# Three wo products between the third and fourth z product, gathers an expert ahead, and pumped work in finer steps spread by VectorE's share

## The chip, the cores and the metric

The kernel runs on one core of a Trainium2 chip. The metric is the device time of one execution in microseconds (us). PE is TensorE (matmuls; PEld is its weight load), DVE is VectorE, ACT is ScalarE, POOL is GpSimd, and SP is the queue that issues most of the DMAs. Instructions of one engine run in the order in which they stand in its program.

## The reference

The input `x` is 8 sequences of 1024 rows of 256 floats. Two blocks follow each other, each added to its input after a layer norm. The first is a gated scan, the second a mixture of experts in which each row goes to two of eight experts, with at most 256 rows for an expert and sequence.

```python
def gated_scan(x):                       # x: [8, 1024, 256], after a layer norm
    h = rmsnorm(x) * gamma
    q, kv, a = split(h @ w_qkva.T, 3)
    y = associative_scan(sigmoid(a), kv) # y[t] = a[t] * y[t-1] + kv[t]
    return q * y

def moe(x):                              # 8 groups of 1024 rows, after a layer norm
    raw = softmax(x @ router_w)          # 8 experts; top 2, capacity 256 a group
    dispatch, combine = gating_top2(raw, C=256)
    inp = einsum('GSEC,GSM->EGCM', dispatch, x)
    hid = gelu(inp @ w0) * (inp @ w1)    # hidden width 1368
    out = hid @ wo
    return einsum('EGCM,GSEC->GSM', out, combine)

x = x + gated_scan(layernorm(x))
x = x + moe(layernorm(x))
```

## The kernel before, in words

**Blocks, units and sets.** The eight sequences are worked in four blocks of two (`n` = 0 to 3). A unit is one expert in one block (`(n, e)`, 32 of them). Its hidden width of 1368 is cut into six sets (`s` = 0 to 5), five of 256 and one of 88. So there are 192 sets, and `run_set` (L836) writes one.

**The products of a set.** The products with `w0` and `w1` are made as one 2x2 block product by seven multiplications instead of eight (Strassen's scheme in Winograd's form). They need sums of weight blocks (`row_sums`, L649, four adds on POOL, written one set ahead), and sums of the gathered inputs (`column_sums`, L632, on DVE, once a unit). Four of the seven are added up in one PSUM bank, `z`, one after the other, and ACT copies the bank out after each of the first three (`sn`, L869, L881, L889); the next product into `z` waits for the copy. `pa` takes one product and `pb` two. L875, L891, L898 and L827 (`first_sum`) on DVE put them together; two gelus stand on ACT (L890, L830). L891 reads `pb` between its first and its second product, and L898 reads `z`, after which the next set may write it. In sets 0 to 4 each of the seven is four PE instructions, in set 5 two.

**The wo products.** The product with `wo` is made by seven multiplications as well (`out_work`, L771), two sets later. They are the work with which `run_set` fills the time that PE would wait: `products()` stands in five places (after the first z, after `pa`, after the second z, after the third z, after the fourth z), and `shares` (L854 to L861) says how many go to each. One such product is two PE instructions (L753). In the set after a set 5 (so in s=1) there are only four. After these, `join_outputs` (L791) adds up the four banks `y0` to `y3` in three parts on DVE; the products of s=2 write the same banks.

**Pumps.** All other work, that of later blocks' scan, norms and gates and the combining of rows of the block before, is cut into steps and handed out by `pump()`, which stands twice in each set: between the first `pb` product and the third z (half 0), and at the set's end (half 1). A block has 96 pumps, and `plan` says which steps each one runs. `unit_steps` (L196) makes the scan's and the norms' steps, `gate_steps` (L322) those of the top-2 gating, `combine_steps` (L483) the fetches and adds of outputs. Steps are spread evenly by their number over the first 88 pumps.

**The bank `aside`.** Steps and `between` that need PE put their result into one PSUM bank, `aside` (`ps_a`, L66): `h_channels`, `x_channels` (four transposes each, then a copy on ACT, L190), `gate_a`, `scan`, `mix` (projections, read by ACT or DVE), `to_tokens` (L270, read by DVE at L276), `router` (L303), `positions` and `tokens`, the transposes of `input_channels` (L627) and those of `output_rows` (L819, the tile `pt_y`).

**Gathers.** `gather_unit` (L609) fetches the rows of a unit by four indirect DMAs from POOL's queue. For the next expert it is called in the first pump of s=0. `between()` (L1021) runs after the fourth z: `input_channels` transposes the gathered rows of the next unit in s=3 and s=4, and `output_rows` writes out the unit before in s=2 and s=5.

In the main loop the order of all engines is the order written (`tc.manual_schedule()`). Ahead of it, up to some 131 us, a first part does the scan and the gates of the first block with only SP's order fixed.

## Time and profile before

| what | value |
|---|---|
| median of 3 runs | 2111.84 us (2111.2 to 2115.47) |
| the profiled execution | 2110.05 us |
| its span, first to last instruction | 2108.2 us |
| mean granted TensorE clock | 0.986 |
| PE busy / PE weight loads busy | 2007.9 / 1609.5 us |
| DVE / ACT / POOL busy | 1370.5 / 681.8 / 1223.4 us |
| DMA moved | 228.87 MB, mean 109 GB/s |

A line of the profile gives the source line, the engine, the operation, what is written and read, the shape and a count. In the timeline the first two numbers are the start and the length in us; runs of equal instructions are merged, and in square brackets stands how long the engine had been idle and what ended that. Matmuls overlap in the pipeline, so the start of one to the start of the next is what it takes of PE. In the list of waits a line gives who waited for whom, the us in total, how often, and the longest.

### The profile page before, as it was taken

Reading aid. Unit: us, or ns where it says so; the run is one execution under the profiler, and the core shown is the slowest. Engines: PE = TensorE matmul, PEld = TensorE weight load, DVE = VectorE, ACT = ScalarE, POOL = GpSimd, SP = SyncE. Lnnn points to the kernel's source line nnn. Section 1 sums busy time; section 2 is a strip of 40 time slices with the busy share of each in tenths; the row PEclk is TensorE's granted clock in tenths of the full one; section 3 lists DMA queues with packets and bytes.
Section 4 is the critical chain, followed back from the end, with each engine's and each line's share of the span. In section 5 each row is a group of like instructions: output and inputs, shape, how many; then the busy total and the mean of one; then the engine's idle time right before and its main releaser. Section 6 shows DMA issues by size and latency. Waiting matters only on the chain.

```text
span 2108.2 us, 27798 instructions
## 1 busy us (share of the span) xinstructions
PE 2007.9 (95%) x9352; PEld 1609.5 (76%) x9352; DVE 1370.5 (65%) x2617; ACT 681.8 (32%) x1286; POOL 1223.4 (58%) x1754
## 2 busy tenths in 40 slices
PE   8899999999999999999999999999999999999958
PEld 4567877777787778787778877787778888878847
DVE  4665666667766575757765666666776667666425
ACT  3333333332333333243233333333323333333311
POOL 3346555546455666657646566666556666767463
PEclk9989999999999999999999999999999999999989
DMA  5223333323224434343423333443333334344351
GB/s 171 80 89 90 91 90 106 103 93 106 78 77 125 115 101 150 88 123 118 123 81 120 109 100 117 120 124 112 111 110 111 116 105 119 100 141 120 97 165 46
DMA packets 224077, 228.87 MB, mean 109 GB/s; under 512 B 32448, under 2 KB 215744, under 8 KB 223936
## 3 DMA queue, kind: packets, MB, share of 16 engines
q1 hardware_dynamic: 211104, 193.51, 31.1%
q0 software_dynamic: 12288, 33.57, 5.4%
q8 instruction: 76, 1.25, 0.3%
q14 instruction: 65, 0.53, 0.1%
q10 hardware_dynamic: 544, 0.01, 0.0%
HBM read 185.61 MB, written 41.42 MB: 108 GB/s over the span
## 4 chain that ended last, share of the span: by engine, by line
PE 85%; DVE 9%; issue 2%; ACT 2%; POOL 1%; DMA 0%; another core or an unknown queue 0%; SPq 0%; ACTq 0%; DVEq 0%; POOLq 0%
PE z L701 29%; PE acc L753 21%; PE pb L701 14%; PE pa L701 7%; PE pa L237 2%; PE pkv L237 2%; PE pq L237 2%; PE py L733 2%; PE px L627 1%; PE pl L303 1%; PE pt_y L819 1%; ACT sn L889 1%; PE po L270 1%; DVE hid L834 1%; PE pc L591 1%
## 5 line engine op out<-in xcount | busy, mean ns | idle before, releaser
L657 POOL TENSOR_TENSOR sb<-w 128x256 f32<-128x256 f32 x188 | 133.0, 708 | 504.9 <-PE pb L701 501.4
L701 PE MATMUL z<-tb,sb 128*128 128x256 f32 (+1 forms) x1408 | 371.8, 383 | 3.3 <-ACT sn L881 3.3
L701 PEld LDWEIGHTS z<-tb,sb 128*128 128x128 f32 (+1 forms) x1408 | 256.1, 187 | 63.9 <-issue 18.2
L891 DVE TENSOR_TENSOR hid<-sn,pb 128x512 f32<-128x512 f32 x192 | 122.6, 639 | 244.0 <-ACT sn L889 206.6
L869 ACT COPY sn<-z 128x512 f32<-128x512 f32 x192 | 105.6, 550 | 439.2 <-PE z L701 409.3
L753 PE MATMUL acc<-tw,so 128*128 128x256 f32 x900 | 244.4, 381 | 0.0
L701 PE MATMUL z<-tb,w 128*128 128x256 f32 (+1 forms) x704 | 200.8, 404 | 40.7 <-ACT sn L889 23.9
L827 DVE TENSOR_TENSOR c<-sn,pb 128x512 f32<-128x512 f32 x192 | 123.1, 641 | 168.5 <-PE pb L701 158.7
L753 PE MATMUL acc<-hid,wo 128*128 128x256 f32 x840 | 216.2, 380 | 0.0
L875 DVE TENSOR_TENSOR c<-sn,pa 128x512 f32<-128x512 f32 x192 | 122.2, 637 | 139.1 <-PE pa L701 129.8
L701 PE MATMUL pb<-xT,sb 128*128 128x256 f32 (+1 forms) x704 | 187.2, 385 | 21.1 <-DVE hid L891 21.1
L889 ACT COPY sn<-z 128x512 f32<-128x512 f32 x192 | 105.6, 550 | 287.9 <-PE z L701 258.2
L881 ACT COPY sn<-z 128x512 f32<-128x512 f32 x192 | 105.6, 550 | 287.4 <-PE z L701 273.0
L701 PEld LDWEIGHTS z<-tb,w 128*128 128x128 f32 (+1 forms) x704 | 118.9, 187 | 99.8 <-ACT sn L889 69.4
L701 PE MATMUL z<-xT,w 128*128 128x256 f32 (+1 forms) x704 | 189.8, 388 | 4.8 <-DVE hid L898 4.6
L701 PE MATMUL pa<-xT,w 128*128 128x256 f32 (+1 forms) x704 | 183.5, 379 | 0.6 <-ACT hT L190 0.6
L701 PE MATMUL pb<-tb,sb 128*128 128x256 f32 (+1 forms) x704 | 183.3, 379 | 0.0
L753 PEld LDWEIGHTS acc<-hid,wo 128*128 128x128 f32 x840 | 160.1, 191 | 23.1
L753 PEld LDWEIGHTS acc<-tw,so 128*128 128x128 f32 x900 | 162.3, 191 | 18.2
L701 PEld LDWEIGHTS pb<-xT,sb 128*128 128x128 f32 (+1 forms) x704 | 130.8, 189 | 47.7 <-DVE hid L891 23.9
L701 PEld LDWEIGHTS z<-xT,w 128*128 128x128 f32 (+1 forms) x704 | 126.2, 188 | 50.3 <-DVE hid L898 20.2
L660 POOL TENSOR_TENSOR sb<-w,sb 128x256 f32<-128x256 f32 x188 | 157.5, 838 | 0.0
(175 smaller groups left out, 3771.0 us busy)
## 6 DMA issues: line engine op xcount, KB each, us to landing
w<-in_L_ffn_w_kernel_dram SPq DMA_DIRECT2D x320, 256.0 KB
wo<-in_L_ffn_wo_kernel_dram SPq DMA_DIRECT2D x160, 256.0 KB
y<-ot SPq DMA_DIRECT2D x62, 256.0 KB
xt<-in_L_attn_x_dram SPq DMA_DIRECT2D x16, 512.0 KB
x<-xt SPq DMA_DIRECT2D x16, 512.0 KB
xn<-xn SPq DMA_DIRECT2D x16, 512.0 KB
xc<-x SPq DMA_DIRECT2D x16, 512.0 KB
out_dram<-xc SPq DMA_DIRECT2D x12, 512.0 KB
```

The costliest lines, as they stand in the source:

```text
L237: nc.tensor.matmul(pp, lhsT=wT[:, k, c * P : (c + 1) * P], rhs=t["hT"][:, k, :], start=(k == 0), stop=(k == KC - 1),)
L657: eng.tensor_tensor(s1, a21, a22, ALU.add)
L660: eng.tensor_tensor(s4, a12, s2, ALU.subtract)
L701: nc.tensor.matmul(ps[:hs, i * CAP : (i + 1) * CAP], lhsT=a[:, i * hs : (i + 1) * hs], rhs=b, start=first and i == 0, stop=True, skip_grou ...
L733: nc.tensor.matmul(po[:, hh * D : (hh + 1) * D], lhsT=st.hid[:hs, gl, i, hh * P : (hh + 1) * P], rhs=wos[st.j][:hs, i, :], start=(s == 0 a ...
L753: nc.tensor.matmul(ys[n, e, i][:, half * CAP : (half + 1) * CAP], lhsT=lhsT, rhs=rhs, start=fresh, stop=True, skip_group_check=True,)
L827: nc.vector.tensor_tensor(st.c12, st.snap1, st.cut(st.pb), ALU.add)
L869: A.copy(snap0, zz)
L875: V.tensor_tensor(c11, snap0, st.cut(p_a), ALU.add)
L881: A.copy(st.snap1, zz)
L889: A.copy(snap2, zz)
L891: V.tensor_tensor(st.h2[: st.hs, 1, st.wide], snap2, st.cut(p_b), ALU.add)
```

## The change

It has four parts. `shares` changes so that three wo products stand after the third z in the usual sets, and one after the fourth; s=1 and s=2 get other shares too, and in s=1 `between()` stands ahead of the fourth z, and `join_outputs(2)` ahead of `first_sum`. The rows of the expert after the next are gathered in the first pump of s=5 (so those of the next one lie ready when a unit begins), and `input_channels` moves from s=3 and 4 to s=1 and 3 in the units where the rows are there in time. Steps are cut finer: both norms into halves, `top`, `counts` and `places` into parts, the one-hots into fours. And each step has a weight for VectorE's time; a pump also has a load from the joins, the column sums and the adds of `combine_steps`, and the steps are handed out so that the running sum of both keeps to an even line.

```diff
-        def first_norm():
+        def first_norm(half):
+            if half == 1:
+                first_rows(half)
+                return
...
-        def second_norm():
+        def second_norm(half):
...
+        def each(w, f):
+            return [weigh(w, lambda c=c: f(c)) for c in range(2)]
+
+        before_mixer = each(12, first_moments) + each(12, first_norm) + each(3, h_channels)
+        mixer = [f for fs in zip(each(5, gate_a), each(13, scan), each(7, mix)) for f in fs]
+        mixer += each(7, to_tokens)
+        after_mixer = each(12, second_moments) + each(10, second_norm) + each(3, x_channels)
+        after_mixer.append(weigh(3, router))
...
-        steps = [softmax, softmax_sum, lambda: top(0), lambda: top(1), counts, positions, places]
+        steps = [weigh(12, softmax), weigh(9, softmax_sum)]
+        steps += [weigh(10, lambda r=r, q=q: top(r, q)) for r in range(2) for q in range(2)]
+        steps += [weigh(13, lambda q=q: counts(q)) for q in range(2)]
+        steps += [weigh(7, positions), weigh(9, places), weigh(9, kept),
+                  weigh(6, output_places), weigh(20, slot_tokens)]
         for gl in range(GB):
-            steps += [lambda gl=gl, q=q: one_hot(gl, q) for q in range(2)]
-            steps.append(lambda gl=gl: tokens(gl))
+            steps += [weigh(13, lambda gl=gl, q=q: one_hot(gl, q)) for q in range(4)]
+            steps.append(weigh(6, lambda gl=gl: tokens(gl)))
...
         if st.s == 1:
-            shares = [2, 2, 0, 0, 0]
+            shares = [1, 2, 1, 0, 0]
...
-            shares = [0, 0, 3, 2, 2] if st.s == 2 else [2, 0, 1, 2, 2]
+            shares = [0, 2, 1, 3, 1] if st.s == 2 else [2, 0, 1, 3, 1]
...
         products()
+        if st.s == 1:
+            between()
         st.mm(z, a22, t4, False)
         V.tensor_tensor(st.h2[: st.hs, 0, st.wide], zz, c11, ALU.mult)
-        between()
+        if joined:
+            join_outputs(*joined, 2)
+        if st.s != 1:
+            between()
         products()
         st.mm(p_b, s4, b22, False)
         first_sum(st)
         if joined:
-            join_outputs(*joined, 2)
             hid_sums(last, 0)
...
+            load = [12 * (k % (2 * NS) in (2, 3)) + 7 * (k % (2 * NS) in (9, 10))
+                    for k in range(PUMPS)]
...
             if n > 0:
                 for i, (fetch, add) in enumerate(combine_steps(n - 1)):
-                    plan.setdefault(13 + i * 14 // 3, []).append(fetch)
-                    plan.setdefault(15 + i * 14 // 3, []).append(add)
+                    at_pump(13 + i * 14 // 3, fetch)
+                    at_pump(15 + i * 14 // 3, add, 11)
+            if n + 1 < NB:
+                steps = list(token_work[n + 2])
+                share = (sum(f.weight for f in steps) + sum(load[: PUMPS - 8])) / (PUMPS - 8)
+                done = 0.0
+                for k in range(PUMPS - 8):
+                    done += load[k]
+                    while steps and done + steps[0].weight / 2 <= share * (k + 1):
+                        done += steps[0].weight
+                        at_pump(k, steps.pop(0))
...
+                later = (n, e + 2) if e + 2 < NE else (n + 1, 1)
+                if half == 0:
+                    if j == 0:
+                        gather_unit(0, 1)
+                    if s == NS - 1 and e + 2 != NE and later in units:
+                        gather_unit(*later)
                 if nxt in units:
-                    if half == 0 and s == 0 and e + 1 < NE:
-                        gather_unit(*nxt)
...
-                if s in (3, 4) and nxt in units:
-                    input_channels(*nxt, s - 3)
+
+                slots = (3, 4) if nxt[1] == 0 or nxt == units[1] else (1, 3)
+                if s in slots and nxt in units:
+                    input_channels(*nxt, slots.index(s))
```

## The prediction

> **What bounds the kernel now.** I read the page first: who is busy and who carries the chain.

> ```profile
> PE 2007.9 (95%) x9352; PEld 1609.5 (76%) x9352; DVE 1370.5 (65%) x2617; ACT 681.8 (32%) x1286; POOL 1223.4 (58%) x1754
> ...
> PE 85%; DVE 9%; issue 2%; ACT 2%; POOL 1%; DMA 0%; another core or an unknown queue 0%; SPq 0%; ACTq 0%; DVEq 0%; POOLq 0%
> ```

> PE carries the chain and runs its program in the order written, so only time in which PE stands still, and PE work itself, move the end. The change adds no PE work. So I looked for where PE stands still: the waits, then the timeline of a unit that has no pumped work (block 3).

> ```profile
> PEld z L701 <- ACT sn L889: 69.4, 152, 1.1
> ...
> PE z L701 <- ACT sn L889: 23.9, 33, 0.7
> ...
> PE pb L701 <- DVE hid L891: 21.1, 17, 3.0
> ...
> PE pt_y L819 <- DVE xt L276: 4.7, 2, 2.4
> ```

> ```profile
> 1621.62 1.03 PE L701 MATMUL z<-tb,sb 128*128 128x256 f32 x4
> 1622.48 1.03 PE L753 MATMUL acc<-tw,so 128*128 128x256 f32 x4
> 1623.38 1.13 PE L701 MATMUL z<-tb,w 128*128 128x256 f32 x4
> 1624.35 0.59 PE L753 MATMUL acc<-tw,so 128*128 128x256 f32 x2
> ...
> 1631.38 1.10 PE L701 MATMUL z<-tb,sb 128*128 128x256 f32 x4
> 1633.21 1.13 PE L701 MATMUL z<-tb,w 128*128 128x256 f32 x4 [0.73 <-ACT sn L889]
> 1634.18 1.03 PE L701 MATMUL pb<-xT,sb 128*128 128x256 f32 x4
> ```

> Starts are what counts: a group x4 lasts 0.86 us from its start to the next one (0.215 an instruction), a wo product (x2) 0.43. In the first set (s=0) two wo products lie between the third and the fourth z product, and from 1621.62 to 1624.35 are 2.73 us where twelve instructions need 2.58: some 0.14 lost at the fourth z, which waits for the ACT copy of the third. In the second set (s=1) nothing lies between: 1.0 lost. Read so, set by set, the timeline gives these stalls of PE: fourth z 0.14 us in 121 sets (s = 0, 2, 3, 4) and 1.00 in each s=1; second z of s=2 0.146 x30; third z of s=1 0.20 x13; first z after s=5 up to 0.54 (19 sets, 7.6 us), after s=1 0.26 (24 sets).

> The rest is VectorE come too late to L891, and here the timeline shows why:

> ```profile
> 1021.15 0.59 PE L753 MATMUL acc<-tw,wo 128*128 128x256 f32 x2
> ...
> 1023.61 0.29 DVE L445 TENSOR_TENSOR tn<-m,kr 128x128 bf16<-128x128 f32 x1
> 1023.82 0.68 DVE L891 TENSOR_TENSOR hid<-sn,pb 128x512 f32<-128x512 f32 x1
> ...
> 1024.55 1.13 PE L701 MATMUL pb<-xT,sb 128*128 128x256 f32 x4 [2.81 <-DVE hid L891]
> ```

> The step `places`, some 20 instructions in one pump, stands ahead of L891. Such stalls: `places` 3.1, 3.1 and 3.4 us at the second pb and 2.6 just behind it; `top`, `one_hot` or an add in a pump of s=1 (1.1, 1.1, 1.0, 0.6, 0.6); and twice `one_hot` (8 instructions), after which the wait for L276 at pt_y and what follows costs 4.1 us each. In s=5 VectorE is late nearly always (12.8 us in 12 sets): that set is short and holds the column sums. All stalls together, summed from the starts, are some 110 us between 131 and 2020 us.

> **The change, part by part.** The sum is made against the profiled execution, 2110.05 us with a span of 2108.2; the median of the runs shown is 2111.84, so I carry the difference over to that.

> *Three products between third and fourth z.* Cover grows from 0.86 to 1.28 us; the wait needed 0.14 more. In 118 sets (the last two units keep their shares) 118 x 0.14 = 16 us gone. What it takes away is one product (0.43) between the fourth z and the next first z, which waits for L898. In a quiet set L898 ends 3.04 us after the last start of the third z, 3.32 with the later fourth z; the next z then comes at 3.66 in s=0 and 4: 0.2 to spare. In about one such set in six VectorE is later than that: 3 us lost. The next nearest wait, second pb for L891, keeps its cover (three products and z in either order).

> *s=2 and s=1 shares.* s=2 gets two products ahead of its second z (0.146 x30 = 4.4 gone; one is left before the third z, 1.28 us of cover where 1.07 is used); s=1 gets one ahead of its third z (0.20 x13 = 2.6 gone). That s=2 may start its products early rests on `join_outputs(2)` coming before `first_sum`. It puts two adds (0.68 each) ahead of L827 on VectorE; behind L827 are the gelu on ACT and the hid sums, and the next L875 comes after the same row of instructions as before. Free; without that cover 0.2 x31.

> *Transposes moved into s=1.* In 27 units (not those before an expert 0, nor the first and the last) the first `input_channels` moves from s=3 to between third and fourth z of s=1: four transposes, 0.43 us from start to start, in a wait of 1.00. 27 x 0.43 = 11.6. Twice the pump just before holds `scan`, whose bank VectorE frees only 1.98 us after PE's last start: there nothing is won but 0.3 lost. I take 10.

> *Gathers an expert ahead.* Four indirect DMAs on POOL (0.98 us and 0.3 between) move from s=0 to the first pump of s=5. The buffers are free by then (second `input_channels` in s=3 or 4). Queued behind them on POOL are row sums for s=1, some 5 us later than now: they end about 4 us before the second z of s=1 wants them. Free; today's row for that wait is `PEld z L701 <- POOL sb L658`, 4.7 us in all, which I hold as its price if the cover is gone. [...] The trace has 128 of these gathers at a mean of 980 ns beside a VectorE that is busy 65%, so nothing is lost; I go by the row.

> *Finer steps, spread by weight.* Steps ahead of one L891 are now at most about 25 weight units (two half moments 2.3 us, or two scaled rows and four one-hots); pumps with that much outside s=1 and s=5 show no stall today. In s=1 at most a scan or an add stays, which stalls 0.08 at most today. Of 12.2 (`places`), 4.6 (s=1) and 8.2 (pt_y) I take 22 as gone. s=5 stays: adds, half norms and `slot_tokens` still fall into its stretch; 0. The SP stores and loads that move with the steps (x1, xn, the next x) are read tens of us later; 0.

> *What spreading by VectorE's share costs.* This is the term that speaks against it. All pumped PE steps, and the transposes of `between`, share one PSUM bank, `aside`. Today each pump holds one step. By weight, a step that is cheap for VectorE (transposes 3, router 3) hardly counts, so they bunch. I worked the plan out from the rule and weights: of 140 pumped steps that use the bank, 40 now stand directly behind another in the same pump, where it was none. Then PE stands until the first one's bank is read:

> ```profile
> 906.51 0.60 PE L187 MATMUL pt_h<-ident,h 128*128 128x128 f32 x4
> ...
> 906.95 1.03 PE L701 MATMUL z<-tb,sb 128*128 128x256 f32 x4
> 907.15 0.59 ACT L190 COPY hT<-pt_h 128x512 f32<-128x512 f32 x1 [0.38 <-PE pt_h L187]
> ```

> Here PE goes on with another bank at 906.95; for the same bank it must await the copy, which ends at 907.74, and a waited-for start costs some 0.15 more (so much lies between a copy's end and the fourth z's start): 0.94 us. Ahead of another stand: h and x transposes 23 times (0.94: 21.6); router 7 (copy done 0.48 after the last start: 0.5 each, 3.5); to_tokens 6 (L276 ends 1.43 after the last start, median: 1.4 each, 8.4); mix 3 (1.1: 3.3); tokens once (0.6). Sum 37. The bounds: nothing, where another wait would have stood there anyway, and 1.9 (the mean of to_tokens, when VectorE is behind) for each, 76; I take 37, each by its own row. [...] By the only such waits that the trace has, at pt_y, one would count none.

> *Pumps left empty.* First z after s=5 waits 0.54 unless the pump before it has PE work; that is now missing in 23 units for 19, and after s=1 in 28 for 24: 3 us lost with rounding up.

> *First 131 us and the end.* Norms in halves change no count of instructions; 0, within 3. The 20 us in which PE stands between 2032 and 2056 lie in the last unit, whose pumps don't change; 0. One product later in its s=1 saves 0.9.

> Sum: 16 + 4.4 + 2.6 + 10 + 22 + 0.9 = 56 won; 3 + 37 + 3 = 43 lost; 13 won. 2111.8 - 12 or 13: 2099.

> **Rivals.** *The bank decides (slower).* One mechanism: bunched steps on `aside`. 56 won against 6 of other losses leaves 50; from 1.25 us a pair the change loses. For: 16 of the pairs are in a pump at the end of a set, where readers on VectorE stand behind L827 and the hid sums, and ACT may be in a gelu (0.63). Against: today's rows are steady at 0.90. At 1.7 a pair: 68 + 6 - 56 = 18 slower, 2130.
> *VectorE stays late.* The steps are finer but the queue is the same, and new heavy pumps or the thinner cover before the next first z take half of the 22 back: 56 - 11 - 43 = 2 won, 2110. For: s=5 is late whatever stands there. Against: the big stalls all follow one long step.
> *The bank is free.* Half of the 40 fall where PE waits anyhow: 56 - 24 = 32 faster, 2080. For: the waits for L898 before a first z are in just those places. Against: they are small (0.26 to 0.54).

> **How the numbers follow.** Forecast 0.58 (faster), bank free 0.08 (faster), VectorE late 0.10 (no change), bank decides 0.24 (slower). A measurement of this kernel can tell 0.2%, about 4 us, from no change. The range 2082 to 2122 leaves out the lower half of "bank free" and the upper half of "bank decides".

> **What would show it.** In the waits after: `z <- ACT sn` at the fourth z nearly gone except in s=1, there about 0.57 each; `pb <- DVE hid` left in s=5; new rows of PE waiting at pt_h, pt_x, pl, po, pq for hT, xnT, logits and xt, some 40 times and 37 us. I am wrong if those rows are far from 37, if fourth z still waits 0.14, or if stalls over 1.5 us at the second pb remain outside s=5.

## The result, and the profile after

The changed kernel takes 2114.29 us (median of 20 runs, 2111.85 to 2119.91), the kernel before 2113.7 beside it (20 runs): a ratio of 1.0008, with a 95% interval of 1.0001 to 1.0015. Within the 0.2% that counts as no change, the time is the same. 2099 was forecast.

The page after, who is busy and who carries the chain:

```profile
PE 2001.1 (95%) x9352; PEld 1628.4 (77%) x9352; DVE 1375.3 (65%) x2617; ACT 683.7 (32%) x1286; POOL 1230.2 (58%) x1754
...
PE 84%; DVE 8%; issue 3%; ACT 2%; DMA 1%; POOL 1%; another core or an unknown queue 1%; SPq 0%; ACTq 0%; DVEq 0%; POOLq 0%
```

Nothing is to be seen here: PE still carries 84% of the chain. The list of waits (who waited for whom, us in total, how often, longest), here for the main loop alone (131 to 2007 us), shows that the waits are others. Source lines have moved: the products of a set are now L737, ACT's copy of the third z is L925, VectorE's L891 and L898 are L927 and L936.

```profile
PE pb L737 <- DVE hid L927: 11.7, 14, 2.3
PE z L737 <- ACT sn L925: 10.0, 27, 0.7
PE po L285 <- ACT xnT L190: 4.7, 7, 0.7
PE z L737 <- DVE hid L936: 3.9, 15, 0.3
PE pt_x L187 <- ACT hT L190: 3.4, 5, 0.7
PE pq L252 <- ACT xnT L190: 3.4, 5, 0.7
PE ptok L498 <- DVE oneh L488: 2.8, 3, 2.1
PE pl L322 <- ACT hT L190: 2.7, 4, 0.7
...
PE pt_h L187 <- DVE xt L291: 2.4, 3, 0.8
PE pa L252 <- DVE xt L291: 2.4, 3, 0.8
```

The rows of `po`, `pt_x`, `pq`, `pl` and `pt_h` are the forecast's new rows, with its partners; `pa` behind `to_tokens` (`xt`) belongs to them, though the forecast didn't name it. The timeline shows the gain and the loss in one set:

```profile
201.32 1.03 PE L737 MATMUL z<-tb,sb 128*128 128x256 f32 x4
202.19 1.46 PE L789 MATMUL acc<-tw,so 128*128 128x256 f32 x6
203.48 1.03 PE L737 MATMUL z<-tb,w 128*128 128x256 f32 x4
...
205.64 0.60 PE L187 MATMUL pt_h<-ident,h 128*128 128x128 f32 x4
206.92 0.65 PE L187 MATMUL pt_x<-ident,xn 128*128 128x128 f32 x4 [0.68 <-ACT hT L190]
208.25 0.65 PE L285 MATMUL po<-ident,oT 128*128 128x128 f32 x4 [0.68 <-ACT xnT L190]
208.74 1.03 PE L737 MATMUL z<-xT,w 128*128 128x256 f32 x4
```

Ten instructions lie between 201.32 and 203.48, 2.16 us, which is 10 x 0.215: the fourth z waits no longer. But each group of transposes comes 1.28 and 1.33 us after the one before, where four take 0.44. Two stalls of 0.84 and 0.89 in one pump give back what a dozen fourth z products have won.

Summed from the starts of PE's instructions, set by set, PE stands in the main loop (from the first set to the last unit) for:

| where PE stands, us | before | after |
|---|---|---|
| fourth z (for ACT's third copy) | 49.1 | 19.5 |
| second and third z | 7.9 | 1.5 |
| second pb (for L891, now L927) | 25.8 | 17.2 |
| first z (for L898, now L936) | 14.6 | 17.7 |
| at a step on the bank `aside` | 5.4 | 39.5 |
| PE's instructions longer at half clock, windows that start in the loop | 6.3 (4) | 11.9 (7) |
| the same, from a window that reaches in from the first part | 0.6 | 2.9 |
| other | 0.9 | 0 |
| sum | 110.6 | 110.2 |

The loop is 1875.5 us long before and 1876.4 after. The rest of the span's 4.0 us lies behind it (101.8 and 104.8 us), in the last unit, on which more is said at the end.

The half clock behind the new stalls is a term that the prediction did not have. One case of it in the timeline and in the table by stretches (busy us and instructions of each engine, then PE's granted clock, DMA share, GB/s):

```profile
222.71 1.85 PE L322 MATMUL pl<-wr,xnT 128*128 128x8 f32 x16
224.83 0.66 PE L285 MATMUL po<-ident,oT 128*128 128x128 f32 x4 [0.28 <-ACT logits L327]
226.27 3.37 PE L252 MATMUL pa<-hT,wT 128*128 128x512 f32 x4 [0.78 <-DVE xt L291]
```

```profile
222.50:226.20 3.70, 2.71 (x22) 2.36 (x20) 1.46 (x3) 0.18 (x1) 1.09 (x2) 0.93 0.00 0
226.20:229.70 3.50, 3.43 (x6) 1.62 (x7) 0.02 (x1) 0.00 (x0) 0.00 (x0) 0.59 0.00 0
```

Three bank steps stand in this pump. In the 3.41 us up to 225.7, PE spends 1.70 us in the router's sixteen small products and stands for 0.83, summed from the starts. Then it has half its clock for 3.41 us (225.7 to 229.1): the wait of 0.78 us ends inside that, and the four products of `gate_a` take 3.2 us from start to start instead of 1.7. What goes ahead of the half clock is looked at under e12.

### The profile page after: what moved, and what is told of

It is laid out like the page before. It is cut to its first block, busy times and chain, and to the rows that moved or that the text cites. A ratio compares the mean times of both kernels' runs of the same rounds, so it can differ in the third digit from the quotient of the medians.

```text
span 2112.2 us, 27785 instructions
## 1 busy us (share of the span) xinstructions
PE 2001.1 (95%) x9352; PEld 1628.4 (77%) x9352; DVE 1375.3 (65%) x2617; ACT 683.7 (32%) x1286; POOL 1230.2 (58%) x1754
## 3 DMA queue, kind: packets, MB, share of 16 engines
q8 instruction: 76, 1.25, 0.2%
## 4 chain that ended last, share of the span: by engine, by line
PE 84%; DVE 8%; issue 3%; ACT 2%; DMA 1%; POOL 1%; another core or an unknown queue 1%; SPq 0%; ACTq 0%; DVEq 0%; POOLq 0%
PE z L737 28%; PE acc L789 21%; PE pb L737 14%; PE pa L737 7%; PE pa L252 2%; PE pq L252 2%; PE pkv L252 2%; PE py L769 2%; PE pl L322 1%; DVE tb L679 1%; PE px L663 1%; PE pt_y L855 1%; ACT sn L925 1%; PE po L285 1%; PE pt_h L187 1%
## 5 line engine op out<-in xcount | busy, mean ns | idle before, releaser
L693 POOL TENSOR_TENSOR sb<-w 128x256 f32<-128x256 f32 x188 | 127.3, 677 | 506.1 <-PE pb L737 505.4
L737 PE MATMUL z<-tb,sb 128*128 128x256 f32 (+1 forms) x1408 | 371.4, 383 | 2.0 <-issue 2.0
L737 PEld LDWEIGHTS z<-tb,sb 128*128 128x128 f32 (+1 forms) x1408 | 262.9, 189 | 56.2 <-issue 18.5
L927 DVE TENSOR_TENSOR hid<-sn,pb 128x512 f32<-128x512 f32 x192 | 122.8, 640 | 219.4 <-ACT sn L925 212.3
L789 PE MATMUL acc<-hid,wo 128*128 128x256 f32 x840 | 222.5, 382 | 0.0
L789 PE MATMUL acc<-tw,so 128*128 128x256 f32 x900 | 221.5, 383 | 0.0
L737 PE MATMUL z<-tb,w 128*128 128x256 f32 (+1 forms) x704 | 188.2, 386 | 27.0 <-ACT sn L925 26.1
L737 PE MATMUL z<-xT,w 128*128 128x256 f32 (+1 forms) x704 | 192.3, 393 | 11.0 <-DVE hid L936 10.2
L925 ACT COPY sn<-z 128x512 f32<-128x512 f32 x192 | 105.4, 549 | 289.4 <-PE z L737 261.4
L737 PE MATMUL pb<-xT,sb 128*128 128x256 f32 (+1 forms) x704 | 184.6, 381 | 13.0 <-DVE hid L927 11.7
L789 PEld LDWEIGHTS acc<-tw,so 128*128 128x128 f32 x900 | 173.3, 193 | 25.3
L737 PE MATMUL pa<-xT,w 128*128 128x256 f32 (+1 forms) x704 | 186.3, 384 | 0.0
L737 PE MATMUL pb<-tb,sb 128*128 128x256 f32 (+1 forms) x704 | 183.6, 379 | 0.0
L737 PEld LDWEIGHTS z<-xT,w 128*128 128x128 f32 (+1 forms) x704 | 128.0, 190 | 58.3 <-DVE hid L936 29.9
L737 PEld LDWEIGHTS z<-tb,w 128*128 128x128 f32 (+1 forms) x704 | 128.8, 188 | 55.3 <-ACT sn L925 36.1
L936 DVE TENSOR_TENSOR hid<-z,c 128x512 f32<-128x512 f32 x192 | 123.7, 644 | 66.2 <-PE z L737 47.6
L737 PEld LDWEIGHTS pb<-xT,sb 128*128 128x128 f32 (+1 forms) x704 | 129.6, 187 | 38.4 <-DVE hid L927 19.1
```

The source lines that it names most:

```text
L693: eng.tensor_tensor(s1, a21, a22, ALU.add)
L737: nc.tensor.matmul(ps[:hs, i * CAP : (i + 1) * CAP], lhsT=a[:, i * hs : (i + 1) * hs], rhs=b, start=first and i == 0, stop=True, skip_grou ...
L789: nc.tensor.matmul(ys[n, e, i][:, half * CAP : (half + 1) * CAP], lhsT=lhsT, rhs=rhs, start=fresh, stop=True, skip_group_check=True,)
L925: A.copy(snap2, zz)
L927: V.tensor_tensor(st.h2[: st.hs, 1, st.wide], snap2, st.cut(p_b), ALU.add)
L936: V.tensor_tensor(st.h2[: st.hs, 0, st.wide], zz, c11, ALU.mult)
```

## The experiments

Numbers "in the loop" below come from the same sum as in the table. e1 to e4 share seven runs of the kernel before (2113.58 us). In the later runs the kernel before takes 2087 to 2089 us, so there ratios and, across the two occasions, loops are compared; the last section says where the difference lies. The expectations call this a difference of chips; but e1 to e4 and e5 to e8 all ran on the chip numbered 5, so only the occasion is known to differ.

**The change in two halves.** `e1_products` is the kernel before with the new shares, the earlier join, the gathers an expert ahead and the transposes in s=1; steps and their spreading are as before. `e2_steps` is the changed kernel with those undone, so that only the finer steps and their spreading by weight are left.

```diff
 # e1_products, on the kernel before (with the gathers and slots of the change)
-            shares = [2, 2, 0, 0, 0]
+            shares = [1, 2, 1, 0, 0]
...
-            shares = [0, 0, 3, 2, 2] if st.s == 2 else [2, 0, 1, 2, 2]
+            shares = [0, 2, 1, 3, 1] if st.s == 2 else [2, 0, 1, 3, 1]
 # e2_steps, on the changed kernel: the same lines the other way round
```

> The kernel before with the new shares, the moved join, the gathers an expert ahead and the transposes in s=1; steps and their spreading stay as before. Theory (the products part is worth what block 3 of the changed kernel shows, where no steps are pumped: 1.08 us a unit): 30 units, 32 us faster, about 2081 us. Rival (in the blocks with pumped work the waits only move to the second pb or the next first z): within 6 us of before.

> The changed kernel with shares, join, gathers and transposes put back: only the finer steps and their spreading by weight. Theory (blocks 0 to 2 of the changed kernel lost what block 3 won): about 32 us slower than before, 2145 us; the waits at the bank aside some 40 us, half-clock windows in the main loop 7 to 9 where before has 4. Rival (the terms as the prediction had them, 22 won, 40 lost): 18 us slower, 2131. Rival (the loss needs both parts): within 6 us of before.

Measured: e1_products 2075.11 us, ratio 0.9830 (0.9807 to 0.9854), 38.5 us faster. e2_steps 2148.33 us, ratio 1.0173 (1.0146 to 1.0200), 34.8 us slower. So the change is two large edits of opposite sign, whose sum (-3.7) is within 5 us of the changed kernel's +0.6. The waits of PE, first of e1_products in its main loop (130 to 1970 us; L891 and L889 are still those of before), then of e2_steps:

```profile
PE pb L701 <- DVE hid L891: 19.9, 16, 3.3
PE z L701 <- ACT sn L889: 9.9, 29, 0.7
```

```profile
PE z L737 <- ACT sn L925: 24.8, 35, 0.9
...
PE pb L737 <- DVE hid L927: 12.5, 15, 2.3
...
PE po L285 <- ACT xnT L190: 4.1, 6, 0.7
```

In e1_products the fourth z waits less and the second pb as before; in e2_steps it is the other way round, and the bank's rows are there. In the loop e1_products loses 73.2 us, and e2_steps 143.4. One part of e2_steps' expectation missed: four half-clock windows start in its loop, two of them of double length, not 7 to 9.

**One step on the bank in a pump.** `e3_one_bank` is the changed kernel whose planner puts at most one step on `aside` into a pump, counts such a step as at least 11 and lets no pump go over 26 units.

```diff
+                def cost(f):
+                    return max(f.weight, 11) if f.bank else f.weight
...
-                    while steps and done + steps[0].weight / 2 <= share * (k + 1):
-                        done += steps[0].weight
...
+                    while steps and done + cost(steps[0]) / 2 <= share * (k + 1):
+                        f = steps[0]
+                        if (held and f.bank) or (now and now + f.weight > 26):
+                            break
...
```

> The changed kernel, but a pump takes at most one step that uses the bank aside and stops at 26 weight units, and such a step counts as at least 11. Theory (the bunched steps and the half-clock windows they bring are the whole loss): 45 to 50 us faster than the changed kernel, about 2066 us; no waits of pt_h, pt_x, po, pq, pa, pl on hT, xnT, logits or xt over 0.2 us. Rival (the same work only waits elsewhere, VectorE being late where steps pile up): within 10 us of the changed kernel.

Measured: 2077.17 us, ratio 0.9831 (0.9815 to 0.9848), some 37 us faster than the changed kernel, not the 45 to 50 expected. The waits of PE in its main loop (133 to 1970 us) hold no row of the bank's above 1.1 us but one, `pos`, a single wait for `counts`:

```profile
PE pb L737 <- DVE hid L927: 14.2, 12, 2.1
PE z L737 <- ACT sn L925: 11.7, 31, 1.1
PE z L737 <- DVE hid L936: 4.0, 15, 0.3
PE pos L409 <- DVE mc L401: 3.3, 1, 3.3
```

In the loop, waits on the bank fall from 39.5 to 5.7 us and the half clock from 11.9 to 4.6 (two windows start there instead of seven). The loop is 40.1 us shorter, and these two terms are 41.1 of it, so the bunching is the cost, and about all of it. The size of the gain fell short because the finer steps are worth less: e3_one_bank is no faster than e1_products, though its steps are fine and those of e1_products coarse (70.8 us lost in the loop against 73.2).

**Spread by number.** `e4_by_count` is the changed kernel with the old rule, each step by its number.

```diff
-                    while steps and done + steps[0].weight / 2 <= share * (k + 1):
-                        done += steps[0].weight
-                        at_pump(k, steps.pop(0))
+                for i, f in enumerate(steps):
+                    at_pump(i * (PUMPS - 8) // len(steps), f)
```

> The changed kernel with its finer steps handed out evenly by their number, as before, not by weight. By the plan 10 steps stand directly behind another on the bank where the changed kernel has 40. Theory (it is the weights that bunch): three quarters of 45 to 50 us faster than the changed kernel, about 2078 us. Rival (it is the finer cutting, with more than one step in a pump, that costs): within 10 us of the changed kernel.

Measured: 2094.79 us, ratio 0.9910 (0.9889 to 0.9931): some 17 us slower than expected. That is 19.5 us faster than the changed kernel, between what the theory (some 36) and the rival (within 10) said. The bank's waits fall to 15.1 us, as ten pairs are left, but three stalls of 3.2 to 3.4 us are new, at the second z. One of them in the timeline:

```profile
415.92 0.29 DVE L363 TENSOR_TENSOR raw<-logits,red 128x128 f32<-128x128 f32 x1
...
416.24 0.31 ACT L364 ACTIVATE raw<-raw 128x128 f32<-128x128 f32 x1 [4.60 <-DVE raw L363]
416.46 0.57 ACT L905 COPY sn<-z 128x512 f32<-128x512 f32 x1
...
417.17 1.17 PE L737 MATMUL z<-tb,sb 128*128 128x256 f32 x4 [2.94 <-ACT sn L905]
```

ACT's part of `softmax` (L364) waits for two operations of VectorE and stands ahead of the copy that the second z needs. So a step that crosses two engines can cost by its place, whatever its weight.

**The wait left in s=1.** In e1_products 17.7 of the 18.9 us at the fourth z lie in s=1. `e5_s1` moves two wo products there.

```diff
-            shares = [1, 2, 1, 0, 0]
+            shares = [0, 1, 1, 2, 0]
```

> e1_products with one more edit: the four wo products of s=1 stand 0, 1, 1, 2, 0 instead of 1, 2, 1, 0, 0, so two of them lie beside the transposes between third and fourth z. In e1_products PE still stands 18.9 us at the fourth z, nearly all of it in the 31 sets s=1, some 0.57 each; two products add 0.86 us of cover. Theory (a product pays where PE waits for ACT's copy, whatever the set): these 18.9 us go, the time falls from 2075 to 2058 (2054 to 2062). Rival (the product is only moved: the second z of s=1, which waits for row sums on POOL, and the third z, which lose one each, now wait instead): 31 x 0.2 to 0.43 come back, 2064 to 2071.

Measured: ratio 0.9715 (0.9698 to 0.9731). The 0.9830 of e1_products holds the longer stretch behind the loop of the first occasion, so the loops are compared: 1820.4 us, 18.6 less. The timeline of the same set, e1_products and then e5_s1:

```profile
823.77 1.03 PE L701 MATMUL z<-tb,sb 128*128 128x256 f32 x4
824.64 0.60 PE L627 MATMUL px<-ident,xg 128*128 128x128 f32 x4
825.53 1.13 PE L701 MATMUL z<-tb,w 128*128 128x256 f32 x4 [0.29 <-ACT sn L889]
```

```profile
817.98 1.03 PE L701 MATMUL z<-tb,sb 128*128 128x256 f32 x4
818.85 1.03 PE L753 MATMUL acc<-hid,wo 88*128 88x256 f32 x4
819.71 0.60 PE L627 MATMUL px<-ident,xg 128*128 128x128 f32 x4
820.15 1.03 PE L701 MATMUL z<-tb,w 128*128 128x256 f32 x4
```

From third to fourth z it is 1.76 us with only transposes between, and 2.17 with two products more, all of it work. The fourth z loses 2.5 us in all now, and neither the second z (0.1) nor the third (0.8) loses more: the theory holds, the rival doesn't.

**VectorE in s=5.** `e6_s5` takes work out of the short set.

```diff
-                    if s == (4, 5)[1 - half]:
+                    early = nxt[1] != 0 and nxt != units[1]
+                    if s == ((3, 4) if early else (4, 5))[1 - half]:
                         column_sums(*nxt, 1 - half)
...
-        elif summed:
+        elif summed and st.s != NS - 1:
             hid_sums(last, 0)
...
+        if summed and not joined and st.s == NS - 1:
+            hid_sums(last, 0)                   # behind L898
```

> e1_products with one more edit: where the gathered rows of the next unit are transposed in s=1 and s=3, column_sums is made one half of a set earlier too (second half of s=3 and first half of s=4 in place of second half of s=4 and first half of s=5... one set earlier each), and in s=5 the hid sums of the set before stand behind L898 and not ahead of it. In e1_products PE stands 16.1 us at first z products (8.8 of it in s=0, behind an s=5) and 12.5 us at the second pb of s=5, each time for VectorE. Theory (VectorE's queue in s=5 is what is late, so taking work out of it moves the end): some 16 to 19 us go, 2056 to 2060. Rival (what leaves s=5 is late in s=3 and s=4 instead, behind whose pumps stands other work): under 8 us go, 2067 to 2075.

Measured: ratio 0.9734 (0.9718 to 0.9750); the loop is 1822.1 us, 17.0 less than in e1_products. The waits:

```profile
PE pb L701 <- DVE hid L891: 13.7, 13, 3.3
...
PE z L701 <- DVE hid L900: 0.7, 1, 0.7
```

L900 is L898 of before; its wait is all but gone. In the loop the first z loses 7.9 us for 16.1, and the second pb of s=5 1.3 for 12.5; 3.0 of that came back in s=4.

**Both.** `e8_both` has both edits.

> Both edits of e5_s1 and e6_s5 on e1_products. Theory (the two waits are in different sets and add up): 2075 less 17 less 17 is 2041 (2036 to 2046). Rival (PE, 95% busy, comes up against the next wait, so the second gain is half): 2046 to 2052.

Measured: ratio 0.9644 (0.9628 to 0.9660), 2012.57 us beside 2086.78. The loop is 1804.1 us, 34.9 less than in e1_products, where the two edits alone gave 18.6 and 17.0: they add up. Its page:

```profile
PE 1965.9 (98%) x9352; PEld 1621.4 (81%) x9352; DVE 1359.7 (68%) x2617; ACT 684.4 (34%) x1286; POOL 1218.1 (61%) x1754
```

**Finer steps on top.** `e9_all` is e3_one_bank with both edits, and the load of the column sums moved along.

> e3_one_bank (the changed kernel with at most one step on the bank aside in a pump) with both edits of e8_both: shares 0, 1, 1, 2, 0 in s=1, column_sums a set earlier, the hid sums in s=5 behind L898. Against e1_products, whose steps are coarse, e3_one_bank lost 7.5 us less at the second pb and 4.6 us more in other waits and half-clock windows. Theory (finer steps are worth what the second pb outside s=5 still loses in e8_both, some 9 us): a ratio to the kernel before of 0.960 (0.957 to 0.963), against 0.9644 for e8_both. Rival (the finer steps give elsewhere what they take here, as in e3_one_bank): 0.963 to 0.967, no better than e8_both.

Measured: ratio 0.9655 (0.9642 to 0.9668), no better than e8_both. The second pb outside s=5 does fall (from 15.3 to 4.0 us), but in s=5 it rises from 1.4 to 9.3, and the bank and the fourth z take 4.6 more. The rival was right: finer steps are more evenly spread, and so some of them now stand in the set that has least room. The version to use is e8_both, whose steps are those of the kernel before.

**The changed kernel again.** `e10_after` is the same program, on the later occasion.

> The changed kernel once more, beside the kernel before. Its main loop took 0.9 us longer than that of before, its span after the loop 3 us longer. If the change itself is worth nothing on any chip: ratio 0.999 to 1.002. If the stalls of 16 to 20 us in the last unit, which the kernel before showed on the chip of the first runs and not on that of e5 to e8, hide a part of it: 0.995 to 0.998 where those stalls are missing.

Measured: 2089.06 us beside 2086.80, ratio 1.0006 (0.9996 to 1.0015). The loop loses 109.9 us, bank 39.6 and seven half-clock windows again, so these are the program's and not the execution's. The stalls in the last unit, which are missing here, hid no gain.

**What goes ahead of the half clock.** Six of the seven windows that start in the loop come 1.6 to 3.2 us after a router's first product, so the router's sixteen products with eight columns were suspected. (The eighth that the expectation counts is the one that reaches in from the first part.) `e12_router_last` puts the router last in its pump.

```diff
+        after_mixer[-1].behind = True           # the router
...
+                for k in set(plan) - {48}:
+                    plan[k].sort(key=lambda f: hasattr(f, "behind"))
```

> The changed kernel with the router step put last in its pump (in one pump, where softmax stands behind it, it stays). The bank aside then serves as many steps in a row as before, and its waits should stay near 39.5 us (a wait of 0.5 us behind a router becomes one of some 0.9 for the router's turn, about 3 us more in seven pumps). But the router's sixteen products with eight columns no longer stand ahead of two waits of PE: six of the eight half-clock windows in the main loop of the changed kernel start 1.6 to 3.2 us after a router's first product. Theory (the half clock comes from waits close together behind those small products): half-clock windows 8 to about 2 or 3, the loss by them 14.8 to 4 to 7 us, the time 4 to 7 us lower: ratio to the kernel before 0.997 to 0.999. Rival (two waits within some 3 us are enough, whatever products lie between): windows 6 to 9, loss 12 to 16 us, the time 2 to 4 us higher: ratio 1.001 to 1.003.

Measured: 2101.42 us beside 2088.74, ratio 1.0065 (1.0053 to 1.0077), slower than even the rival said. The theory's forecast fell: seven windows start in the loop, four of them twice as long where it was one, and the loss rises from 11.9 to 17.1 us; waits on the bank rise from 39.5 to 46.1. In the waits:

```profile
PE pl L322 <- DVE xt L291: 6.2, 5, 2.2
```

The router now waits for `to_tokens`, 1.4 us a time (7.0 us in five, from the starts), where `to_tokens` waited 0.43 for the router. Putting the router last brought no gain. But the rival (two waits, whatever products lie between) doesn't hold either: the waits of 0.84 and 0.89 us at 206.92 and 208.25 us, shown first, were followed by no half clock (the granted clock is 1.00 from 206 to 222 us).

**The stall in the last unit.** `e7_half_tail` and `e11_half_tail` were to test the 19 us in which PE stands in the last unit.

> The kernel before, leaving out the fetch and the add of the second expert's rows in the last block's combining (14 to 16 indirect DMAs from POOL and as many adds on VectorE fewer). In the last unit PE stands for some 19 us (2032 to 2056 us in the kernel before) while POOL issues about 28 indirect DMAs back to back; the wait named is one of ACT for PE, whose own work had long ended. Theory (PE's stall is held up by the burst of indirect DMAs on POOL): the stall follows their number, so about half of it goes, 8 to 12 us, and the end with fewer adds a few us more: 2098 to 2106. Rival (PE waits for something else, such as a step of VectorE): the stall stays at 19 us and the time at 2108 to 2114.

> e7_half_tail once more (the kernel before, leaving out the fetch and the add of the second expert's rows in the last block's combining). On a chip where the kernel before takes 2111 to 2116 us, it has stalls of some 19 us in its last unit. Theory (they follow the burst of indirect DMAs on POOL): a part goes with half of the DMAs, ratio 0.994 to 0.997. Rival (PE waits for something else): ratio 0.999 to 1.001. Where the kernel before takes 2087 us the stall is not there, and the run tells nothing of it.

Measured: ratios 1.0001 (0.9991 to 1.0010) and 0.9995 (0.9985 to 1.0004), both where the stall was not there. They tell nothing of its cause.

## Why the prediction was wrong

Which waits go and which come, and between which partners, was right. The step that failed is in *What spreading by VectorE's share costs*: each new stall was priced by its own length, as if the products after it kept their pace, and the half clock that came with the bunched stalls was put at nothing. The new half-clock windows cost 11.9 us, and the one from the first part 2.3 more: 14.2 us, more than the 13 that were forecast as won.

*The products* (16 + 4.4 + 2.6 + 10 + 0.9 won, 3 lost at the first z; 31 net): e1_products is 38.5 faster. Right, a little low: the fourth z lost 30 us less, where 16 + 10 were summed, and the first z lost 1.5 more instead of 3. Moving the gathers and the join cost nothing that shows: the second z, for which the row sums are wanted, lost 4.5 us before and 0.1 after.

*The finer steps* (22 won): right in size. Second pb, the bank's waits of before (at `pt_y`) and other fell by 8.6, 5.4 and 0.9, 15 together. The prediction's 12.2 us for `places` and 8.2 for the two stalls at `pt_y` with "what follows" are some 14 us of standing and 6 of half clock behind it. So the four windows of before (6.3 us), which follow these stalls and are gone, belong to this term: 21 us in all. Within it "s=5 stays; 0" was wrong: it lost some 2 to 3 us more. e9_all shows it at its clearest, with 1.4 going to 9.3 where fine steps meet the emptied set.

*The bank* (37 lost): 39.5, but by another sum; that it came so near is luck. 39 pairs can be seen, and they cost 31.2 us: the transposes that went before another step 0.84 each for 0.94, router 0.43 for 0.5, `to_tokens` 0.93 for 1.4, `mix` 0.93 for 1.1. The other 8 are no pairs of the count: 2.8 is `tokens` directly behind its own one-hots. Every one of the 39 pairs was a stall, and with one step in a pump (e3_one_bank) they were gone.

*The half clock* (not in the sum for the new stalls): 11.9 us in the seven windows that start in the loop, six of which follow a router in a bunched pump, and 2.3 more from one that reaches in from the first part. e3_one_bank gives back 7.3 in the loop with the pairs. In the case shown above no wait that ended before the half clock began was over 0.42 us (from the starts), and the clock is halved for 3.41 us.

*Empty pumps and the end* (3 lost, 0.9 won, first part and end 0): the first z lost 3.1 more in all, where 3 + 3 were summed. Behind the loop 3.0 were lost in the profiled execution, in its stall of the last unit. The first part was put at 0, within 3: in the traces with coarse steps the loop starts at 130.1 to 130.9 us, with finer steps at 131.1 to 136.1, so up to 5 us can go there.

So, from the table: 36.0 won at the fourth, third and second z, 14.9 and 6.3 by the finer steps; 39.5 lost at the bank, 3.1 at the first z and 14.2 by the new half clock; 0.4 won in all. Against the 13 forecast, the half clock took 14, the bank 2.5 and the finer steps 1, while the products and the first z together gave some 5 more. A pair cost 0.80 us by itself, not the 1.25 from which the rival had the bank decide; with the half clock and the bank's other waits, spreading cost 53.7 us, 1.34 for each of the 40 pairs counted.

## What to carry to other kernels

Two edits that each move 35 us were tied together here; a sum whose terms cancel to a third of one of them says little, and each half should be measured alone. When work is spread by one engine's load, the planner must know what else a step holds: steps that are nothing to VectorE still took turns on a PSUM bank here (0.80 us a pair), and a step split over ACT and VectorE still held up the copies behind it (2.94 us in the case shown of e4_by_count). And after a wait is covered in the usual case, look for the sets where it is not: s=1 and s=5 held 35 us that took a few lines. Short stalls close together cost more than their length here: the changed kernel's loop has 39.5 us of waits on the bank and 11.9 of half clock, that of e3_one_bank 5.7 and 4.6.

## What the runs showed of the hardware

Ahead of each half-clock window in the loops of `before` and `after`, PE's standing and the router's products of eight columns came to 2.21 to 2.90 us of a stretch of 3.413 us; in no other stretch at full clock did they come to more than 2.09. Over all 14 traces the two kinds overlap, from 1.99 to 2.18 us. This is a sum counted in these loops; why the clock was halved no run shows, and whether other small products count was not measured. In the case shown no wait that had ended was over 0.42 us, and the same program had seven such windows in its loop in both of its traces. The windows of 3.41 us cost 1.3 to 1.7 us each in the changed kernel.

In the last unit, on the occasion of the first runs, PE stood still for 16 us. It went on when ACT had made its copy of the third z; but ACT had been idle for 19 us by then and VectorE for 22.6, and nothing in the trace ends ACT's idle time. The granted clock is halved there as well (2043.3 to 2060.4 us). Of the kernel before:

```profile
2038.15 1.90 PE L733 MATMUL py<-wo,hid 128*128 128x256 f32 x4
...
2055.40 0.59 ACT L889 COPY sn<-z 128x512 f32<-128x512 f32 x1 [19.07 <-issue]
...
2056.02 0.69 DVE L891 TENSOR_TENSOR hid<-sn,pb 128x512 f32<-128x512 f32 x1 [22.55 <-issue]
...
2056.04 2.08 PE L701 MATMUL z<-tb,w 128*128 128x256 f32 x4 [15.98 <-issue]
```

On the later occasion (e10_after) the changed kernel's same place has no wait beyond the usual:

```profile
2038.68 1.03 PE L769 MATMUL py<-wo,hid 128*128 128x256 f32 x4
2039.58 1.13 PE L737 MATMUL z<-tb,w 128*128 128x256 f32 x4
```

The span behind the loop is 104.8 us on the one and 76.8 on the other for the same program, with loops of 1876.4 and 1876.0. By the medians the kernel before was 27 us faster on the later occasions, the changed one 25. POOL issues some 28 indirect DMAs in a row at that time, but it does so in e10_after as well (2027 to 2062 us) while PE goes on. So the row of DMAs alone does not bring the stall; its cause stays open.
